# Seven stages instead of ten for a tile of rows through its expert, shifts on GpSimd, a second load

## The chip, the cores and the metric

The kernel runs on one core of one Trainium2 chip. The metric is the time of one execution on the device, in microseconds; the median of several runs is compared.

In the text, TensorE is the matrix engine (PE in the profile, PEld its loading of weights), VectorE is DVE, ScalarE is ACT, GpSimd is POOL, and SyncE (SP) issues most transfers. Each engine works through its own queue in order; where an instruction needs something of another engine or of a transfer, it waits, and everything behind it in that queue waits too.

## What is computed

Two layers over 6250 rows of 512 numbers: a graph layer (mean over incoming edges, two products, a norm over all rows, relu), and a mixture of eight experts of which each row uses two.

```python
x = x + gnn(layernorm(x), edge_index, W_l, b_l, W_r, gamma, beta)
x = x + ffn(layernorm(x)[None], ...)[0]

# gnn(x):
agg = segment_sum(x[src], dst)
h = (agg / maximum(cnt, 1)[:, None]) @ W_l.T + b_l + x @ W_r.T
h = (h - mean(h, 0)) * rsqrt(var(h, 0) + EPS) * gamma + beta
return relu(h) + x

# ffn(t):  D, H, E, K = 512, 256, 8, 2
logits = gelu(t @ Wg1 + bg1) @ Wg2 + bg2
topv, topi = top_k(softmax(logits), K);  topv = topv / sum(topv)
h = einsum('td,edh->eth', t, W1) + b1[:, None]
h = gelu(ln(h, g1, be1))
h = einsum('eth,ehg->etg', h, W2) + b2[:, None]
h = gelu(ln(h, g2, be2))
o = einsum('eth,eho->eto', h, W3) + b3[:, None]
out = einsum('te,eto->to', cw, o)      # cw: the two weights of a row
```

## The kernel before

**First part (to about 1226 us of the profile).** Rows are normalised and written to memory, edges are gathered by indirect transfers, summed by products with selection matrices, and multiplied with W_l and W_r. The change does not touch it.

**Tokens.** The 6250 rows are 49 tiles of 128 ("tokens"), in seven groups of seven. For each tile: two loads (`token_load`), the batch norm on VectorE (`token_scale`, L822 and L823), the residual on ScalarE (`token_shift`, L828), the sum and its statistics on VectorE (`token_sum`, L834 and L784), which also stores the sum to `out` as the value to which the experts will add (L835), the layer norm on ScalarE (`token_norm`, L804), transposes (`token_turn`, L846), and the gate (`token_gate`, `token_logits`). The two groups that come first are done ahead of the experts (`ahead`); the others go along with them, at most one tile in a step.

**Routing.** `route(q)` is a generator that finds for a group the two experts of each row, their weights (with an exponential on ScalarE, L920) and a slot for each, in pieces on VectorE that are put into the steps (`do`, `late`). Rows are then scattered by GpSimd (`send`, L868) to `xs_d`, a list of tiles of 128 rows, each tile of one expert. A row in `xs_d` has 528 columns (RW): 512 values, the row's number, eight weights and padding.

**Experts.** There are 102 tiles of slots in the main run (MOST), each through ten stages. `run(s, ...)` is one step. It issues, in this order of the program and so of every queue:

| place in a step | function, line | tile | engine |
|---|---|---|---|
| loads, four tiles ahead | `job_load` L1071 | to s+3 | SP |
| turn of the rows, copy to `xT` | `job_turn` L1086, L1088 | s | TensorE, ScalarE |
| turns of normed layers, gelu | `layer_turn` L1113, L1116 | s-3, s-6 | TensorE, ScalarE |
| scatter-add to `out` | `job_out` L1140 | s-9 | GpSimd |
| bias of W3 | `job_bias` L1132 | s-8 | VectorE |
| token work of VectorE | `token_scale`, `token_sum` | | VectorE |
| shifts of the last step's statistics | `shifts` L799 | | VectorE |
| norms | `layer_norm` L804 | s-2, s-5 | ScalarE |
| weighing | `job_weigh` L1136 | s-8 | ScalarE |
| pieces of the routing, row scatters | `do` | | VectorE, GpSimd |
| W1, its bias, statistics | `layer` L1096, L1099, L784 | s-1 | TensorE, VectorE |
| W2, its bias, statistics | `layer` | s-4 | TensorE, VectorE |
| W3 | `job_product` L1125 | s-7 | TensorE |
| a token's turn and gate | L846, L855 | | TensorE |
| scales | `scales` L794, L795 | | VectorE, GpSimd |

The order is written out by hand (`tc.manual_schedule`). A norm needs a scale, (var + EPS)^-0.5, and a shift, -mean times the scale. `scales`, at the end of a step, adds EPS on VectorE (L794) and takes the power on GpSimd (L795). `shifts`, in the middle of the next step, makes the product on VectorE (L799). `mv` holds them, three columns (tokens, first layer, second layer) by three numbers.

`job_turn` also copies the row's number, as an integer, and the weight of the tile's expert out of the loaded tile `xe` (four buffers) into `to` and `cw` (14 buffers each); the scatter takes `to` as its offsets, the weighing `cw` as its factor. `oe` has three buffers. Scatter-adds to `out` are in order: each waits for the one before it to land, as two tiles may hold the same row. After the last tile, ten more steps empty the stages.

Of the kernel before, what the change touches and what calls it, by code (L numbers as in the profile page):

```python
# [28 lines left out]
def gnn_moe_kernel(ctx: ExitStack, tc: tile.TileContext, x, src, dst, wlT, b_l, wrT, gamma, beta,  # L29
# [736 lines left out]
    def no_tokens(a):  # L766

        nc.vector.memset(a, 0.0)
        nc.vector.memset(a[:, D:D + 1], OOB)
        return a  # L770

    JOBS = {}

    class Step:
# [14 lines left out]
        def scales(self):  # L789
            if self.used:  # L790
                lo, hi = min(self.used), max(self.used) + 1
                assert hi - lo == len(self.used)
                self.part = self.mv[:, lo:hi]
                nc.vector.tensor_scalar(self.part[:, :, 1], self.part[:, :, 1], EPS, None, op0=OP.add)  # L794
                nc.gpsimd.tensor_tensor(self.part[:, :, 1], self.part[:, :, 1], mhalf[:, :hi - lo], op=OP.pow)  # L795

        def shifts(self):
            if self.used:
                nc.vector.scalar_tensor_tensor(self.part[:, :, 2], self.part[:, :, 0], -1.0,  # L799
                                               self.part[:, :, 1], op0=OP.mult, op1=OP.mult)  # L800
                self.used = []
# [80 lines left out]
    def route(q):  # L882
# [36 lines left out]
        nc.vector.tensor_tensor(s[:, 2:4], s[:, 0:2], s[:, None, 0].to_broadcast([P, 2, n]), op=OP.subtract)  # L919
        nc.scalar.activation(s[:, 2:4], s[:, 2:4], AF.Exp)  # L920
# [4 lines left out]
        nc.vector.tensor_copy(t2[:, :n, D], tok[:, g[0]:g[0] + n])  # L925
# [6 lines left out]
        nc.vector.tensor_add(s[:, 0], s[:, 2], s[:, 3])  # L932
        nc.vector.reciprocal(s[:, 1], s[:, 0])
        nc.vector.tensor_tensor(s[:, 2:4], s[:, 2:4], s[:, None, 1].to_broadcast([P, 2, n]), op=OP.mult)
# [131 lines left out]
    def job_load(p):  # L1066
        sl, e = JOBS[p]
        at = nc.values_load(sl, engines=[SP_], min_val=0, max_val=SLOTS,
                            skip_runtime_bounds_check_because="a tile's number, or SLOTS")
        xe = sb.tile([P, RW], F32, name="xe", bufs=4)  # L1070
        ld = nc.sync.dma_start(xe, xs_d[ds(at, 1)].rearrange("o p c -> p (o c)"))  # L1071
        tc.add_to_no_dep_group("full", ld.ins)
        XE[p] = xe

    def job_turn(p):
        xe = XE.pop(p)
# [69 lines left out]

    flat = [(q, j) for q in range(NQ) for j in range(len(groups[q]))]
# [14 lines left out]
    def ahead(i):  # L1162
# [10 lines left out]
        if i:  # L1173
            STEP[i - 1].shifts()
# [21 lines left out]
    def run(s, prev, lo, hi, moves=False, do=(), late=()):  # L1196
# [28 lines left out]
        tprev.shifts()  # L1225
        prev.shifts()
        for lag in (2, 5):
# [42 lines left out]
    with tc.manual_schedule():  # L1270
# [31 lines left out]
        STEP[n - 1].shifts()  # L1302
# [9 lines left out]
        tprev.shifts()  # L1312
# [53 lines left out]
        for s in range(MOST, MOST + 10):  # L1366
            prev = run(s, prev, 0, MOST)
    with tc.If(flag > 0), tc.manual_schedule():
        prev = Step()
        for s in range(MOST, SLOTS + 10):  # L1370
# [38 lines left out]
```

## Time and profile before

| what | us |
|---|---|
| median of 6 runs | 2039.19 (2034.93 to 2047.4) |
| the profiled execution | 2032.26 |
| its span, first to last instruction | 2030.5 |
| first turn of a tile in the expert part | 1309.90 |
| first scatter-add of results | 1375.98 |
| last turn of a tile | 1966.41 |
| last scatter-add | 2020.12 |

Busy time of each engine in stretches of the expert part, in us, with the clock granted to TensorE as a share of full speed:

| stretch | length | TensorE | VectorE | ScalarE | GpSimd | clock | DMA share |
|---|---|---|---|---|---|---|---|
| 1310 to 1340 | 30 | 22.98 | 25.47 | 13.81 | 7.27 | 0.67 | 0.50 |
| 1340 to 1375 | 35 | 33.78 | 23.75 | 22.44 | 13.27 | 0.92 | 0.44 |
| 1380 to 1752 | 372 | 352.40 | 304.00 | 271.41 | 189.96 | 0.98 | 0.68 |
| 1752 to 1838 | 86 | 73.72 | 58.55 | 49.36 | 55.22 | 0.95 | 0.61 |
| 1838 to 2031 | 193 | 157.81 | 94.49 | 105.16 | 75.39 | 0.92 | 0.44 |

A line of the page's groups gives the source line, the engine, the operation, output and input, the count, then busy time and the mean of one, then the engine's idle time just before and what ended it. A line of the timeline gives start, duration, engine, line, and in brackets the idle time ahead of it. A line of the waits gives who waited for whom: total, times, longest.

### The profile page before, as it was taken

The numbers are of one execution on the slowest core, as the hardware profiler recorded it, in microseconds if no ns is written. First come the engines' busy times: TensorE is split into PE (matmuls) and PEld (weight loads), VectorE is DVE, ScalarE is ACT, GpSimd is POOL, SyncE is SP. The second block draws the span as 40 slices with busy tenths as digits, with TensorE's granted clock in tenths as the row PEclk, the third lists the DMA queues.
The fourth block names the chain that finished last, engine by engine and source line by source line (L and its number), as shares of the span: only waits on it lengthen the run. The fifth ranks groups of instructions, "written<-read, shape, count | busy, mean of one in ns | idle before, by whom it ended". The sixth has DMA issues, their size and how long they took to land. (4 is left out here: it accounts for less than half of the span.)

```text
span 2030.5 us, 23976 instructions
## 1 busy us (share of the span) xinstructions
PE 1863.8 (92%) x6268; PEld 1033.3 (51%) x6268; DVE 1091.0 (54%) x2577; ACT 667.9 (33%) x1284; POOL 1212.0 (60%) x1229
## 2 busy tenths in 40 slices
PE   5877999999999999999999995588999999989993
PEld 2433444444444444444444443366767676666761
DVE  5652434334434434343344336878787878765661
ACT  3420101101010001011010014457777777756662
POOL 1427777777777777777777751335454646474442
PEclk9988999999999999999999996589999999999997
DMA  7968888878788888889888765646676767566532
GB/s 248 300 213 275 256 241 244 250 240 249 243 241 256 278 259 274 260 269 311 280 265 286 239 194 183 210 171 168 170 190 162 207 147 200 105 154 122 96 59 35
DMA packets 183185, 434.09 MB, mean 214 GB/s; under 512 B 32484, under 2 KB 38638, under 8 KB 182626
## 3 DMA queue, kind: packets, MB, share of 16 engines
q0 software_dynamic: 91040, 274.90, 49.0%
q1 hardware_dynamic: 91606, 156.69, 22.9%
q8 instruction: 56, 0.92, 0.2%
q10 hardware_dynamic: 396, 0.87, 0.1%
q14 instruction: 87, 0.71, 0.1%
HBM read 331.22 MB, written 104.20 MB: 214 GB/s over the span
## 5 line engine op out<-in xcount | busy, mean ns | idle before, releaser
L636 POOL DMA_INDIRECT xg<-xn_d,scol x832 | 795.1, 956 | 260.0 <-issue 123.9
L643 PE MATMUL pa<-xg,sel 128*128 128x512 f32 x1664 | 788.0, 596 | 20.7 <-DMA y_d<-xg 18.0
L643 PEld LDWEIGHTS pa<-xg,sel 128*128 128x128 f32 x1664 | 306.3, 190 | 364.4 <-issue 350.5
L1140 POOL DMA_INDIRECT out<-oe,to x102 | 165.6, 1624 | 196.6 <-DMA out<-oe,to 45.0
L528 ACT ACTIVATE sq<-dt 128x512 f32<-128x512 f32 x49 | 29.5, 602 | 557.4 <-DVE dt L526 281.2
L795 POOL TENSOR_TENSOR mv<-mv,mhalf 128x2 f32<-128x2 f32 (+2 forms) x121 | 106.1, 877 | 178.2 <-DVE mv L794 163.9
L1096 PE MATMUL pm<-w1s,xT 128*128 x816 | 207.8, 400 | 4.8 <-DVE hn L1099 4.8
L1125 PE MATMUL po<-w3s,hT 128*128 x408 | 197.4, 607 | 12.7 <-DVE oe L1132 12.4
L562 DVE TENSOR_REDUCE ss<-sel 128x128 f32<-128x2304 f32 x49 | 200.5, 4092 | 0.6 <-issue 0.6
L432 PE MATMUL ph<-wl,xT 128*128 128x512 f32 x392 | 199.8, 592 | 0.7 <-ACT xT L427 0.7
L1096 PEld LDWEIGHTS pm<-w1s,xT 128*128 128x128 f32 x816 | 154.6, 200 | 25.1 <-DVE hn L1099 5.9
L1116 ACT ACTIVATE hT<-pt,gbe 128x128 f32<-128x128 f32 x408 | 154.2, 462 | 1.9 <-PE pt L1113 1.8
L507 DVE TENSOR_SCALAR rc<-pt 128x1 f32<-128x1 f32 x49 | 7.8, 158 | 270.7 <-PE pt L586 270.7
L804 ACT ACTIVATE hn<-hn,mv 128x256 f32<-128x256 f32 x204 | 111.9, 599 | 108.0 <-DVE mv L799 107.7
L868 POOL DMA_INDIRECT xs_d<-t,pos x98 | 101.6, 1037 | 40.8 <-issue 23.8
L556 DVE TENSOR_TENSOR sel<-jrow_p,dcol 128x2304 f32<-128x2304 f32 x49 | 124.4, 2539 | 0.0
L432 PEld LDWEIGHTS ph<-wl,xT 128*128 128x128 f32 x392 | 74.4, 190 | 94.2 <-issue 93.3
L526 DVE TENSOR_TENSOR dt<-ph,shift 128x512 f32<-128x512 f32 x25 | 17.3, 692 | 192.2 <-PE ph L432 192.2
L567 ACT ACTIVATE ag<-pa,rc 128x512 f32<-128x512 f32 x49 | 33.7, 687 | 248.9 <-PE pa L643 248.9
L1125 PEld LDWEIGHTS po<-w3s,hT 128*128 128x128 f32 x408 | 76.2, 192 | 75.8 <-issue 53.9
L524 DVE TENSOR_TENSOR dt<-ph,xo 128x512 f32<-128x512 f32 x24 | 16.6, 692 | 182.4 <-PE ph L432 182.4
L1096 PE MATMUL pm<-w2s,hT 128*128 x408 | 104.8, 379 | 0.0
(307 smaller groups left out, 2246.0 us busy)
## 6 DMA issues: line engine op xcount, KB each, us to landing
xe<-xs_d SPq DMA_DIRECT2D x102, 264.0 KB
xg<-xn_d,scol POOLq DMA_INDIRECT x832, 3.9
d_d<-dt SPq DMA_DIRECT2D x49, 256.0 KB
dt<-d_d SPq DMA_DIRECT2D x49, 256.0 KB
xt<-in_x SPq DMA_DIRECT2D x24, 512.0 KB
xn_d<-xt SPq DMA_DIRECT2D x24, 512.0 KB
xy<-y_d SPq DMA_DIRECT2D x48, 256.0 KB
xt<-in_x SPq DMA_DIRECT2D x48, 256.0 KB
```

Source lines behind the costliest of these rows:

```text
L432: nc.tensor.matmul(p, xT[:, k, :], w[:, k, :], start=start and k == 0, stop=stop and k == KD - 1)
L556: nc.vector.tensor_tensor(SEL[t], jrow_p[:, None, :].to_broadcast([P, KS, P]), dcol[:, t // TG, (t % TG) * KS:(t % TG + 1) * KS, None].to_ ...
L562: nc.vector.tensor_reduce(ss, SEL[t].rearrange("p k j -> p j k"), AX.X, OP.add)
L636: nc.gpsimd.indirect_dma_start(out=xg, out_offset=None, in_=xn_d[:, :], in_offset=bass.IndirectOffsetOnAxis(ap=scol[:, t // TG, c:c + 1], ...
L643: nc.tensor.matmul(PA[t], SEL[t][:, k, :], xg, start=(k == 0), stop=(k == last))
L795: nc.gpsimd.tensor_tensor(self.part[:, :, 1], self.part[:, :, 1], mhalf[:, :hi - lo], op=OP.pow)
L804: nc.scalar.activation(out_, in_, AF.Identity, bias=scale_shift[1], scale=scale_shift[0])
L868: st = nc.gpsimd.indirect_dma_start(out=xs_d.rearrange("n p c -> (n p) c"), out_offset=bass.IndirectOffsetOnAxis(ap=at, axis=0), in_=rows_ ...
L1096: nc.tensor.matmul(pm, lhs[:, k, :], w[:, k, ds(e, 1), :].rearrange("p o h -> p (o h)"), start=(k == 0), stop=(k == kk - 1))
L1116: nc.scalar.activation(hT[:, k, :], pt[:, k, :], AF.Gelu, bias=gb[:, 2 * i + 1:2 * i + 2], scale=gb[:, 2 * i:2 * i + 1])
L1125: nc.tensor.matmul(po, hT[:, k, :], w3s[:, k, ds(e, 1), :].rearrange("p o h -> p (o h)"), start=(k == 0), stop=(k == KH - 1))
L1140: st = nc.gpsimd.indirect_dma_start(out=out[:, :], out_offset=bass.IndirectOffsetOnAxis(ap=to[:, 0:1], axis=0), in_=OE.pop(p), in_offset=N ...
```

## The change

Stages are drawn together: W1 is issued in the step of its turn (tile s), W2 in the step of its turn (s-2), W3 goes ahead of W1 and W2 (s-5), and its bias and weighing follow in the same step. The second turn is of tile s-4, the scatter-add of s-6. Seven steps empty the stages, not ten.

The shift is made on GpSimd behind the power, as is the addition of EPS; VectorE only negates the mean. `shifts` is gone.

The loaded tile comes in two transfers: 512 values into `xe`, the last 16 columns into `ev` (14 buffers), which the scatter and the weighing read directly; the row's number is stored there as an integer from the start. The two copies are gone.

The exponential of the routing is a power of e on GpSimd, of one number instead of two. The tile without tokens, written once at the start, uses another buffer.

```diff
@@ no_tokens
-        nc.vector.memset(a[:, D:D + 1], OOB)
+        nc.vector.memset(a[:, D:D + 1].bitcast(I32), int(OOB))
...
+    euler = wts.tile([P, GMAX], F32, name="euler")
+    nc.vector.memset(euler, 2.718281828459045)
@@ Step.scales
-                nc.vector.tensor_scalar(self.part[:, :, 1], self.part[:, :, 1], EPS, None, op0=OP.add)
-                nc.gpsimd.tensor_tensor(self.part[:, :, 1], self.part[:, :, 1], mhalf[:, :hi - lo], op=OP.pow)
-
-        def shifts(self):
-            if self.used:
-                nc.vector.scalar_tensor_tensor(self.part[:, :, 2], self.part[:, :, 0], -1.0,
-                                               self.part[:, :, 1], op0=OP.mult, op1=OP.mult)
-                self.used = []
+                mean, var, shift = (self.part[:, :, i] for i in range(3))
+                nc.vector.tensor_scalar(shift, mean, -1.0, None, op0=OP.mult)
+                nc.gpsimd.tensor_scalar(var, var, EPS, None, op0=OP.add)
+                nc.gpsimd.tensor_tensor(var, var, mhalf[:, :hi - lo], op=OP.pow)
+                nc.gpsimd.tensor_tensor(shift, shift, var, op=OP.mult)
@@ route
-        nc.vector.tensor_tensor(s[:, 2:4], s[:, 0:2], s[:, None, 0].to_broadcast([P, 2, n]), op=OP.subtract)
-        nc.scalar.activation(s[:, 2:4], s[:, 2:4], AF.Exp)
+        nc.vector.tensor_sub(s[:, 3], s[:, 1], s[:, 0])
+        nc.gpsimd.tensor_tensor(s[:, 3], euler[:, :n], s[:, 3], op=OP.pow)
...
-        nc.vector.tensor_add(s[:, 0], s[:, 2], s[:, 3])
-        nc.vector.reciprocal(s[:, 1], s[:, 0])
-        nc.vector.tensor_tensor(s[:, 2:4], s[:, 2:4], s[:, None, 1].to_broadcast([P, 2, n]), op=OP.mult)
+        nc.vector.tensor_scalar(s[:, 0], s[:, 3], 1.0, None, op0=OP.add)
+        nc.vector.reciprocal(s[:, 2], s[:, 0])
+        nc.vector.tensor_mul(s[:, 3], s[:, 3], s[:, 2])
@@ job_load
-        xe = sb.tile([P, RW], F32, name="xe", bufs=4)
-        ld = nc.sync.dma_start(xe, xs_d[ds(at, 1)].rearrange("o p c -> p (o c)"))
-        tc.add_to_no_dep_group("full", ld.ins)
-        XE[p] = xe
+        xe = sb.tile([P, D], F32, name="xe", bufs=4)
+        ev = sb.tile([P, RW - D], F32, name="ev", bufs=14)
+        for a, lo, hi in ((xe, 0, D), (ev, D, RW)):
+            ld = nc.sync.dma_start(a, xs_d[ds(at, 1), :, lo:hi].rearrange("o p c -> p (o c)"))
+            tc.add_to_no_dep_group("full", ld.ins)
+        XE[p] = xe, ev
@@ job_turn
-        to = sb.tile([P, 1], I32, name="to", bufs=14)
-        cw = sb.tile([P, 1], F32, name="cw", bufs=14)
-        nc.vector.tensor_copy(to, xe[:, D:D + 1])
-        nc.vector.tensor_copy(cw, xe[:, D + 1:D + 1 + E][:, ds(e, 1)])
-        EV[p] = e, to, cw
+        EV[p] = e, ev[:, 0:1].bitcast(I32), ev[:, 1:1 + E][:, ds(e, 1)]
@@ ahead
-        if i:
-            STEP[i - 1].shifts()
@@ run
-        for i, lag in ((0, 3), (1, 6)):
+        for i, lag in ((0, 2), (1, 4)):
             if on(lag):
                 layer_turn(s - lag, i)
-        if on(9):
-            job_out(s - 9)
-        if on(8):
-            job_bias(s - 8)
+        if on(6):
+            job_out(s - 6)
...
-        tprev.shifts()
-        prev.shifts()
-        for lag in (2, 5):
+        if on(5):
+            job_product(s - 5)
+            job_bias(s - 5)
+        for lag in (1, 3):
             if on(lag):
                 layer_norm(s - lag)
...
-        if on(8):
-            job_weigh(s - 8)
+        if on(5):
+            job_weigh(s - 5)
         for f in do:
             f()
-        if on(1):
-            layer(s - 1, 0, step)
-        if on(4):
-            layer(s - 4, 1, step)
-        if on(7):
-            job_product(s - 7)
+        if on(0):
+            layer(s, 0, step)
+        if on(2):
+            layer(s - 2, 1, step)
@@ the start of the token work
             if i == 3:
-                no = sb.tile([P, RW], F32, name="xe", bufs=4)
-                nc.sync.dma_start(xs_d[SLOTS], no_tokens(no))
+                nc.sync.dma_start(xs_d[SLOTS], no_tokens(t2s[1][:, 0, :]))
@@ the last steps
-        for s in range(MOST, MOST + 10):
+        for s in range(MOST, MOST + 7):
             prev = run(s, prev, 0, MOST)
```

More of the change, by code (lines that the diff above doesn't have):

```diff
@@ L924, in route @@
         nc.vector.tensor_add(m, mm[:, 0], mm[:, 1])
-        nc.vector.tensor_copy(t2[:, :n, D], tok[:, g[0]:g[0] + n])
+        nc.vector.tensor_copy(t2[:, :n, D].bitcast(I32), tok[:, g[0]:g[0] + n])
         nc.vector.memset(t2[:, :, D + 1 + E:], 0.0)
@@ L1069, in job_load @@
                             skip_runtime_bounds_check_because="a tile's number, or SLOTS")
[L1070 to L1073 removed]
+        xe = sb.tile([P, D], F32, name="xe", bufs=4)
[4 more added lines that the diff above has]
+        XE[p] = xe, ev
     def job_turn(p):
[L1076 removed]
+        xe, ev = XE.pop(p)
         e = nc.values_load(JOBS[p][1], engines=[PE_, DVE_, ACT_], min_val=0, max_val=E - 1,
                            skip_runtime_bounds_check_because="an expert's number")
[L1079 to L1083 removed]
+        EV[p] = e, ev[:, 0:1].bitcast(I32), ev[:, 1:1 + E][:, ds(e, 1)]
         pt = ps.tile([P, KD, P], F32, name="pt", bufs=3)
@@ L1301, in gnn_moe_kernel @@
         token_scale(*flat[n])
-        STEP[n - 1].shifts()
         token_norm(*flat[n - 1])
@@ L1311, in gnn_moe_kernel @@
         token_scale(*flat[n + 1])
-        tprev.shifts()
         token_norm(*flat[n])
@@ L1369, in gnn_moe_kernel @@
         prev = Step()
-        for s in range(MOST, SLOTS + 10):
+        for s in range(MOST, SLOTS + 7):
             prev = run(s, prev, MOST, SLOTS)
```

## The prediction

> **What bounds the kernel now.** I read the page first, then the last part of the chain of waits, the scatter's own rows, one undisturbed step of TensorE, and last what TensorE and ScalarE waited for. The change touches the expert part, which begins with the first turn of a tile at 1309.90 us, and a little of the token work from 1226 on; the sums before that stay.
>
> The end is set by the scatter-adds of results. The page's group, the scatter's landing, and the last rows of GpSimd's timeline (start, duration, idle time before and what ended it):
>
> ```profile
> L1140 POOL DMA_INDIRECT out<-oe,to x102 | 165.6, 1624 | 196.6 <-DMA out<-oe,to 45.0
> ```
> ```profile
> DMA to landing us min/median/max: 3.1/5.0/7.6
> ```
> ```profile
> 1999.88 1.59 POOL L1140 DMA_INDIRECT out<-oe,to  x1 [3.22 <-DMA out<-oe,to]
> 2005.47 1.53 POOL L1140 DMA_INDIRECT out<-oe,to  x1 [4.00 <-DMA out<-oe,to]
> 2010.60 1.53 POOL L1140 DMA_INDIRECT out<-oe,to  x1 [3.60 <-DMA out<-oe,to]
> 2016.27 1.54 POOL L1140 DMA_INDIRECT out<-oe,to  x1 [4.14 <-DMA out<-oe,to]
> 2020.12 1.54 POOL L1140 DMA_INDIRECT out<-oe,to  x1 [2.32 <-DMA out<-oe,to]
> ```
>
> Each scatter starts about 0.77 us after the one before has landed: the scatters are a chain of their own, whoever has finished earlier. Scatter 68 starts at 1838.10, scatter 101 at 2020.12: 182.0 us for 33, or 5.52 us each. From scatter 55 (1757.88) on it is 5.70 each, and most already follow on the landing. The last tile is turned at 1966.41, so 53.7 us are drain.
>
> One step without tokens, on TensorE, in the same stretch:
>
> ```profile
> 1864.19 0.60 PE L1086 MATMUL pt<-identx,xe 128*128 128x128 f32 x4
> 1864.63 0.60 PE L1113 MATMUL pt<-identx,hn 128*128 128x128 f32 x4
> 1865.06 1.89 PE L1096 MATMUL pm<-w1s,xT 128*128 x8
> 1866.79 1.03 PE L1096 MATMUL pm<-w2s,hT 128*128 x4
> 1867.65 1.88 PE L1125 MATMUL po<-w3s,hT 128*128 x4
> ```
>
> It repeats every 5.18 us without a gap, slightly faster than the scatters' 5.52; they fall behind it and at last hold it up. With tokens a step takes 7.26 us (turns at 1614.31, 1621.56, 1628.82), and there TensorE leads. From 1380 to 1752 it is busy 352.40 of 372 us. What it waited for from 1380 to 1890, and ScalarE's longest wait from 1380 on:
>
> ```profile
> PE pt L846 <- ACT t L804: 12.0, 6, 2.8
> PE pt L1113 <- ACT hn L804: 6.0, 6, 2.0
> ```
> ```profile
> ACT hn L804 <- DVE mv L799: 104.6, 59, 4.8
> ```
> ```profile
> 1592.72 0.82 ACT L828 ACTIVATE xt<-xt,nm,mr 128x512 f32<-128x512 f32 x1
> 1596.26 1.09 ACT L804 ACTIVATE hn<-hn,mv 128x256 f32<-128x256 f32 x2 [2.72 <-DVE mv L799]
> ```
>
> The reader is to see that the norms wait for VectorE's shift (L799), which is queued behind the next step's token work, although GpSimd had its power ready at 1592.77.
>
> **The change, part by part.**
>
> *Ten stages to seven.* In step s the scatter of tile s-6 is issued, not of s-9. The place in GpSimd's queue is the same: ahead of the row scatters and the scales. So at any late step the chain of scatters is three tiles ahead, and 3 x 5.52 = 16.6 us fall off the end. Bounds: 15.5 (TensorE's 5.18 a step decides) and 17.1 (5.70).
>
> *Cost of filling.* The tiles in flight are done earlier, so TensorE has more behind it at any step: one W1 (1.72), two W2 (0.87 each), two W3 (1.72 each), two tiles' second turn and one tile's first (three times 0.43, half of the four transposes' 0.87): 1.72 + 1.74 + 3.44 + 1.3 = 8.2 us. It hides in idle time of TensorE while the pipe fills: 7.0 us from 1310 to 1340 (busy 22.98 of 30, at a granted clock of 0.67) and 1.2 to 1375. VectorE is busy 25.47 of the first 30 us and stretches those steps. Without cover it costs 8.2; covered, nothing. I take 3, since 8.2 of idle time stand against work that the clock of 0.67 makes longer.
>
> *Order within a step.* W3 now lies between the turns and W1. The copy of xT takes 0.59 and ends 1.28 us after the turn's start (1864.88 against 1864.19); W1 starts at 0.87 + 1.72 = 2.6. The two gelus of the first layer end some 0.75 later and W2 starts at 4.3. So W1 and W2 need not wait: nothing, with 1.3 us to spare. Bias and weighing go behind W3 in the same step: W3 ends near 2.7, bias 0.69, weighing 0.7, done at 4.1 of 5.18; in VectorE's queue the bias goes behind the token work (four operations of 0.68 to 0.69), and the scatter that needs it comes a step later. What loses cover is the norm: before, W3's 1.72 us lay between W2's end and the next step. From W1's end (1861.77) to the power's start (1864.45) it is 2.7 us. In the new step W1 ends 0.7 before the next turn, so GpSimd starts 2.0 after it.
>
> *Shifts on GpSimd.* VectorE loses the shift (0.15 us) and swaps adding EPS for a negation. GpSimd gets an add and a product, not seen in the trace. Nearest row, the power: 0.54 us for one column, 0.70 for two, 0.88 for three, and 1.15 directly behind a scatter. Some 0.17 a column is the power's own work, so 0.37 is the lower bound, 0.88 the upper, 1.15 behind a scatter. I take 0.5, as an add is cheaper than a power. Then the scales are ready at 2.0 + 0.5 + 0.7 + 0.5 = 3.7 in the pure step; ScalarE gets there at 2.56, ends two norms (1.10) and the weighing (0.73) at 5.6, and its next copy is due at 5.87. Nothing on the path, by 0.3 us; beyond that, xT still has 1.3 us of W3's cover. In token steps nothing waits for VectorE's queue any more: at 1592.77 + 1.0 the norms could start at 1593.8 instead of 1596.26. Of the 18.0 us of TensorE's waits above I take 8 back (0 to 18), as some will turn into waits for GpSimd.
>
> The power beside VectorE's product of two SBUF tiles (L822) took 0.75 us at 1586.10, against 0.72 at 1864.45 with none beside it. The Trainium skill, "SBUF — State Buffer", section "SBUF: two separate sides", says that a GpSimd operation and a VectorE operation with two SBUF inputs exclude each other for the whole instruction. By that rule each of the two new operations could wait 0.69 us, so the scales come 1.4 us later in a token step, about half of what the norms win there; 8 would shrink to 4 and the sum would be -14.6. By the row it stays as taken.
>
> *GpSimd in the last group.* From 1752 to 1838 it is busy 55.22 of 86 us, scatters and rows alternate, and the chain of waits goes through its row scatters. Two more operations of 0.5 in 13 steps, hidden where a landing is waited for: 0 to 8 us, I take 3, because most of those scatters still started 0.77 to 0.82 after a landing.
>
> *A second load.* SP issues 102 small loads more. The queue's packets average 22.9% x 16 x 2030.5 / 91606 = 81 ns; 128 of them on 16 engines are 0.65 us of each engine per tile, 9 points of DMA share. Landings take about 5.1 at shares of 0.6 to 0.7 and 4.8 in the drain at 0.44, so 0.1 us a scatter: 0 to 4 us over the 43 that bind, I take 2. In return the xe buffer is freed by TensorE alone; SP waited 172.9 us for the copy (L1082), at a lead of 10 to 20 us, so no gain. The two copies (0.15 each) leave VectorE, which is not the bound: nothing.
>
> *Softmax as a power on GpSimd, token steps before the experts.* ScalarE loses 14 table loads of 1.28 us, of which two or three lie on the path (TensorE idled 1.79 us at 1285.57 behind one). VectorE, busy 16 to 19 of every 20 us from 1240 to 1300, loses 17 shifts of 0.15; against it stands 1.0 us more from sum to norm at the end of two runs of tokens. I take -2 (-5 to +2).
>
> Sum: -16.6 + 3 - 8 + 3 + 2 - 2 = -18.6 us. The profiled execution took 2032.26 us (span 2030.5 and 1.8 around it), so it would take 2013.7. The median of the runs shown, 2039.19, lies 6.9 above that execution; the forecast for the median is 2020.6 us.
>
> **The rivals.**
>
> *More than that.* All 18 us of the norms' waits come back, the fill is free, the small costs vanish: -16.6 - 18 - 5 = -39.6, 1999.6 us. For it speaks that 59 waits for L799 go; against it, that the token steps have other edges (xe cost 4.9 once).
>
> *It evens out.* The fill costs its 8.2, nothing comes back at the norms: -16.6 + 8.2 + 2 + 3 + 2 = -1.4, 2037.8 us. For it speaks TensorE's 352 of 372 busy.
>
> *GpSimd becomes the bound (slower).* In a token step its queue holds 0.74 from a landing to the scatter's start, the scatter 1.62, two row scatters of 1.0 with 0.3 ahead of each, and the power 0.94: 5.9 of 7.26 us. The two new operations fit while they are below 0.68 each. At 1.15 each, the row behind a scatter, the step is 0.9 too long; 70 row scatters make 35 such steps, 33 us: -18.6 + 33 = +14.4, 2053.6 us. Against it: behind row scatters the power took 0.94, hardly more than alone.
>
> **How the numbers follow.** The forecast gets 0.55, the larger gain 0.14, evening out 0.13, GpSimd 0.18. The forecast's own range is 2010 to 2032; taking in the bounds of fill and norms and both milder rivals, 2001 to 2040, which leaves out nearly all of the slower case and half of the larger gain's low end. About 0.3%, 6.1 us, is what a measurement can tell from none: faster, below 2033.1, is the forecast, the larger gain and a little of evening out: 0.72; same 0.10; slower 0.18.
>
> **What would show it.** Right: the last scatter comes some 37 us after the last turn, not 53.7; scatters stay 5.5 apart; ScalarE's norms no longer wait for VectorE; pure steps stay at 5.18. Wrong: pure steps above 5.3 with TensorE waiting for hn (the norms have lost their cover), token steps above 7.3 with GpSimd busy throughout, or scatters above 5.7 apart in the drain (the small loads). The tail's 16.6 fails if scatters are held by something else than the landing.

## The result and the profile after

The changed kernel takes 2052.82 us (median of 20 runs, 2043.99 to 2057.24) against 2039.3 of the kernel before on the same chip (46 runs): ratio 1.0061, 95% interval [1.0049, 1.0073]. The forecast was 2020.6 and a gain.

The two profiled executions, cut at the same points (starts of the tiles' turns, L1086 before and L1083 after; the last product of L432 ends a part that the change doesn't touch). A profile is of one execution: 2032.26 us before, 7.0 below its median, and 2051.13 after, 1.7 below, so the table's sum of 18.9 is more than the 13.5 between the medians. The untouched part alone lies between 1221.6 and 1227.0 in the fourteen profiles that are not of e10 to e13 (whose chip is slow there, see below).

| stretch | before, us | after, us | difference |
|---|---|---|---|
| start to the last product of L432 | 1222.4 | 1225.7 | +3.3 |
| to the first turn (token work alone) | 87.5 | 94.9 | +7.4 |
| turn 0 to turn 10 (fill) | 68.5 | 73.3 | +4.8 |
| turn 10 to turn 64 | 373.3 | 388.9 | +15.6 |
| turn 64 to turn 101 (last) | 214.7 | 217.4 | +2.7 |
| last turn to last scatter (drain) | 53.7 | 39.1 | -14.6 |
| last scatter to the end | 10.4 | 10.1 | -0.3 |
| span | 2030.5 | 2049.4 | +18.9 |

The drain came near its forecast (14.6 us shorter, 16.6 expected). The page's group of the scatter-add and the last scatters on GpSimd's timeline (start, duration, idle time ahead and what ended it):

```profile
L1137 POOL DMA_INDIRECT out<-oe,ev x102 | 167.2, 1639 | 159.5 <-ACT hn L803 35.0
```
```profile
2024.35 1.63 POOL L1137 DMA_INDIRECT out<-oe,ev  x1 [2.82 <-DMA out<-oe,ev]
2029.91 1.55 POOL L1137 DMA_INDIRECT out<-oe,ev  x1 [3.93 <-issue]
2035.39 1.55 POOL L1137 DMA_INDIRECT out<-oe,ev  x1 [3.93 <-issue]
2039.27 1.55 POOL L1137 DMA_INDIRECT out<-oe,ev  x1 [2.33 <-POOLq L1358]
```

They are still some 5.5 apart (5.68 each from scatter 68 to 101, where it was 5.52). But the chain starts later: the turns have lost 23 us on their way from the first to the last, and 7 before it. What TensorE, VectorE and ScalarE waited for in the changed kernel from 1310 to 1960 (total us, times, longest), one engine after the other:

```profile
PE pt L845 <- ACT t L803: 26.1, 21, 3.1
PE pt L1110 <- ACT hn L803: 12.4, 13, 1.9
PE pl L928 <- DVE t L925: 5.1, 4, 1.5
```
```profile
DVE oe L1129 <- PE po L1122: 94.7, 53, 7.9
```
```profile
ACT hn L803 <- POOL mv L800: 130.4, 78, 4.0
```

In the same stretch of the kernel before, TensorE's first two waits were 18.6 and 6.2 us, and ScalarE's norms waited 92.1 us for the shift. So the norms do not wait less; they wait more, and for GpSimd. (How much of that is the shifts' new place is seen only in e1 and e9.) New is that VectorE stands 94.7 us in front of W3's bias (L1129). What that does is seen best where tokens end, in a step that all groups have. TensorE of the changed kernel from turn 21 to turn 22, then VectorE:

```profile
1473.36 0.66 PE L1083 MATMUL pt<-identx,xe 128*128 128x128 f32 x4
1474.70 1.98 PE L1122 MATMUL po<-w3s,hT 128*128 x4
1476.52 1.89 PE L1093 MATMUL pm<-w1s,xT 128*128 x8
1478.25 1.03 PE L1093 MATMUL pm<-w2s,hT 128*128 x4
1480.48 0.40 PE L928 MATMUL pl<-gm,lower 128*128 128x56 f32 x2 [1.21 <-DVE t L925]
1480.94 0.61 PE L1083 MATMUL pt<-identx,xe 128*128 128x128 f32 x4
```
```profile
1473.95 0.17 DVE L797 TENSOR_SCALAR mv<-mv 128x2 f32<-128x2 f32 x1
1476.78 0.69 DVE L1129 TENSOR_TENSOR oe<-po,b3s 128x512 f32<-128x512 f32 x1 [2.66 <-PE po L1122]
1477.39 0.21 DVE L910 TENSOR_REDUCE gs<-pl 128x7 f32<-128x56 f32 x1
...
1480.12 0.22 DVE L923 TENSOR_TENSOR gm<-gmm 128x56 f32<-128x56 f32 x1
```

VectorE has nothing to do for 2.66 us, because the next thing in its queue is the bias of W3, and W3 has only begun (1474.70); the routing (L910 to L925), whose input is there, starts 4.03 us after the turn. Before, the bias stood at the head of the step and the routing started 1.44 after it. Its mask reaches TensorE late, and the step is 7.58 long in place of 6.13. There are five such steps (8-9, 21-22, 35-36, 49-50, 63-64): 7.57, 7.58, 7.58, 7.58, 7.85 against 6.13 each, 7.5 us together.

The norms, in the step from 1641.83 on, GpSimd, then ScalarE, then TensorE:

```profile
1642.31 1.65 POOL L1137 DMA_INDIRECT out<-oe,ev  x1 [3.93 <-ACT tt L847]
1644.27 1.44 POOL L867 DMA_INDIRECT xs_d<-t,pos  x1 [0.30 <-issue]
1646.01 0.99 POOL L867 DMA_INDIRECT xs_d<-t,pos  x1 [0.31 <-issue]
1647.00 0.30 POOL L798 TENSOR_SCALAR mv<-mv 128x3 f32<-128x3 f32 x1
1647.38 0.89 POOL L799 TENSOR_TENSOR mv<-mv,mhalf 128x3 f32<-128x3 f32 x1
1648.35 0.19 POOL L800 TENSOR_TENSOR mv<-mv 128x3 f32<-128x3 f32 x1
1648.58 1.09 ACT L803 ACTIVATE hn<-hn,mv 128x256 f32<-128x256 f32 x2 [3.23 <-POOL mv L800]
1650.43 0.66 PE L845 MATMUL pt<-identx,t 128*128 128x128 f32 x4 [2.69 <-ACT t L803]
```

The statistics were ready at 1641.66 (the negation, L797). The scatter ahead in GpSimd's queue had itself waited 3.93 us, then came two row scatters, and only 5.3 us after the statistics the three small operations. They are cheap (0.30, 0.89, 0.19); what costs is where they stand.

The same is seen without tokens. Steps without tokens begin at 5.18 us, but from turn 86 to turn 99 they last 5.35 to 5.77 (in e1, with the shifts on VectorE, they are 5.18 up to turn 94). In the step from 1928.51 the statistics are ready at 1930.34, GpSimd stands at a scatter that starts at 1931.03, the three operations end at 1934.00, and the norm starts at 1934.03; TensorE, nowhere idle for long, is held up at the second turn (0.93 us in place of 0.60).

### The profile page after: what moved, and what is told of

Read it like the earlier page. It is cut to its first block, busy times and chain, and to the rows that moved or that the text cites. A ratio compares the mean times of both kernels' runs of the same rounds, so it can differ in the third digit from the quotient of the medians.

```text
span 2049.4 us, 24603 instructions
## 1 busy us (share of the span) xinstructions
PE 1866.9 (91%) x6268; PEld 1030.6 (50%) x6268; DVE 1048.2 (51%) x2251; ACT 650.6 (32%) x1263; POOL 1293.3 (63%) x1472
## 5 line engine op out<-in xcount | busy, mean ns | idle before, releaser
L1137 POOL DMA_INDIRECT out<-oe,ev x102 | 167.2, 1639 | 159.5 <-ACT hn L803 35.0
L1122 PE MATMUL po<-w3s,hT 128*128 x408 | 203.0, 621 | 1.6 <-DVE oe L1129 1.6
L432 PE MATMUL ph<-wl,xT 128*128 128x512 f32 x392 | 199.8, 592 | 0.7 <-ACT xT L427 0.7
L1093 PE MATMUL pm<-w1s,xT 128*128 x816 | 197.0, 385 | 3.7 <-DVE hn L1096 2.0
L1129 DVE TENSOR_TENSOR oe<-po,b3s 128x512 f32<-128x512 f32 x102 | 70.6, 692 | 133.3 <-PE po L1122 122.9
L432 PEld LDWEIGHTS ph<-wl,xT 128*128 128x128 f32 x392 | 74.4, 190 | 94.2 <-issue 93.3
L798 POOL TENSOR_SCALAR mv<-mv 128x2 f32<-128x2 f32 (+2 forms) x119 | 48.0, 403 | 111.7 <-DVE mv L787 111.4
L524 DVE TENSOR_TENSOR dt<-ph,xo 128x512 f32<-128x512 f32 x24 | 16.6, 692 | 184.2 <-PE ph L432 184.2
```

The source lines that it names most:

```text
L432: nc.tensor.matmul(p, xT[:, k, :], w[:, k, :], start=start and k == 0, stop=stop and k == KD - 1)
L1093: nc.tensor.matmul(pm, lhs[:, k, :], w[:, k, ds(e, 1), :].rearrange("p o h -> p (o h)"), start=(k == 0), stop=(k == kk - 1))
L1122: nc.tensor.matmul(po, hT[:, k, :], w3s[:, k, ds(e, 1), :].rearrange("p o h -> p (o h)"), start=(k == 0), stop=(k == KH - 1))
L1129: nc.vector.tensor_add(oe, OE[p], b3s[:, ds(e, 1), :].rearrange("p o h -> p (o h)"))
L1137: st = nc.gpsimd.indirect_dma_start(out=out[:, :], out_offset=bass.IndirectOffsetOnAxis(ap=to[:, 0:1], axis=0), in_=OE.pop(p), in_offset=N ...
```

## The experiments

Two theories. *Queue*: W3's bias, now in the middle of VectorE's queue, holds up what stands behind it (the shifts if they are there, and the routing). *Cover*: W3 no longer lies behind W2 and gives the norms no time. Rivals: the scales' place in GpSimd's queue, the routing's power, the second load.

"Prelude" is from L432's last product to the first turn, "way" from the first turn to the last, "drain" from there to the last scatter, each from one profile; ratios are to the kernel before on the same chip. The profiled execution is not the median one: it took 11 us more than the median in e8, 7 in e2, 6 in e6 and 20 in e10 (in all four the slowest), 16 less in e13 and 4 less in e1. No kernel was profiled twice, so a difference of a few us between two rows is not told from chance.

| run | ratio, 95% interval | prelude | way | drain |
|---|---|---|---|---|
| before | 1 | 87.5 | 656.5 | 53.7 |
| changed | 1.0061 [1.0049, 1.0073] | 94.9 | 679.6 | 39.1 |
| e1 shifts back | 1.0036 [1.0022, 1.0051] | 88.0 | 672.2 | 38.4 |
| e2 Exp back | 1.0050 [1.0033, 1.0068] | 90.6 | 688.0 | 37.5 |
| e4 ten stages | 1.0072 [1.0053, 1.0091] | 91.8 | 664.5 | 53.3 |
| e5 stages alone | 1.0056 [1.0040, 1.0072] | 86.8 | 681.8 | 38.6 |
| e6 shifts first | 1.0051 [1.0032, 1.0069] | 90.1 | 681.5 | 38.8 |
| e7 W3 first | 1.0142 [1.0115, 1.0168] | 89.8 | 676.3 | 53.2 |
| e8 eight stages | 0.9946 [0.9927, 0.9965] | 91.1 | 661.3 | 43.2 |
| e9 shifts alone | 1.0068 [1.0044, 1.0092] | 92.7 | 665.0 | 52.7 |
| e10 bias late | 0.9946 [0.9906, 0.9987] | 93.7 | 671.4 | 37.9 |
| e11 bias late, shifts back | 0.9982 [0.9949, 1.0016] | 90.2 | 664.7 | 36.9 |
| e12 eight, load, power | 0.9877 [0.9827, 0.9927] | 88.6 | 653.5 | 41.8 |
| e13 load alone | 0.9944 [0.9912, 0.9977] | 91.0 | 655.9 | 52.7 |
| e14 W3 first, bias late | 1.0075 [1.0060, 1.0089] | 89.6 | 671.2 | 53.3 |
| e15 eight, load | 0.9915 [0.9895, 0.9935] | 87.6 | 653.3 | 42.8 |
| e16 seven mended | 0.9987 [0.9977, 0.9996] | 87.6 | 665.4 | 38.4 |
| e17 W2 last | 1.0058 [1.0042, 1.0074] | 87.8 | 666.9 | 50.3 |

Four chips: the kernel before took 2030.8 (e1 to e5), 2031.7 (e6 to e9), 2232.0 (e10 to e13) and 2033.1 us (e14 to e17). On the third, nearly all of the excess lies ahead of L432's last product (1396 to 1434 us in the four profiles, in place of 1222), so those four ratios are blunt; the expert part takes no longer than elsewhere (e13), and its stretches are compared. The prelude scatters by 2 us either way in runs that change nothing in it (86.8 to 91.1).

### One part taken back at a time (e1, e2, e4, e5)

*e1, shifts and EPS on VectorE again*

```diff
-nc.vector.tensor_scalar(shift, mean, -1.0, None, op0=OP.mult)
-nc.gpsimd.tensor_scalar(var, var, EPS, None, op0=OP.add)
-nc.gpsimd.tensor_tensor(var, var, mhalf[:, :hi - lo], op=OP.pow)
-nc.gpsimd.tensor_tensor(shift, shift, var, op=OP.mult)
+nc.vector.tensor_scalar(self.part[:, :, 1], self.part[:, :, 1], EPS, None, op0=OP.add)
+nc.gpsimd.tensor_tensor(self.part[:, :, 1], self.part[:, :, 1], mhalf[:, :hi - lo], op=OP.pow)
...
+        tprev.shifts()
+        prev.shifts()
         for lag in (1, 3):
```

> The changed kernel with the shifts and the adding of EPS on VectorE again; the power alone stays on GpSimd. If the scales' new place is the cause (all three operations in GpSimd's queue, behind a scatter that waits for its landing and behind the row scatters; ScalarE's hn waited 152.8 us for POOL mv L800), the steps before the last group lose some 15 to 20 us and the time falls to about 2035, with turn 64 some 462 us after the first turn in place of 442 before and 462 now turning back to about 445. If the order of the stages is the cause (W3 at the start of the step has taken the norm's cover), it stays at 2045 to 2055. If the routing's power is the cause, it stays at about 2045 to 2050.

2038.44 us. It lands between: 5 us better in the ratio, not 15 to 20, and the two intervals just touch. Nor did the steps before the last group come back: turn 64 is 465.5 us after the first turn (462.2 in the changed kernel, 445 expected). What is shorter is the last group, 206.7 against 217.4, and the prelude.

*e2, the exponential on ScalarE again*

```diff
-nc.gpsimd.tensor_tensor(s[:, 3], euler[:, :n], s[:, 3], op=OP.pow)
+nc.scalar.activation(s[:, 3], s[:, 3], AF.Exp)
```

> The changed kernel with the softmax's exponential on ScalarE again. If the routing's power in GpSimd's queue is the cause (17.9 us in which GpSimd stood at L919 waiting for VectorE, and 7 us of the way to the first turn), the time falls by 15 to 20 us, to about 2035. If the scales' place is the cause, it falls by 5 at most, by what the first turn comes earlier (about 2048). If the order of the stages is, by 5 at most too.

2043.99 us; the intervals of this ratio and the changed kernel's overlap. The routing's power is not the cause.

*e4, ten stages in the old order, all else as changed* (lags 3, 6, 9, 8 and W1, W2, W3 at the step's end, as in the kernel before)

> The changed kernel with ten stages again, in the order of before; all else as changed. The drain grows by 14 to 17 us. If the order of the stages is what lengthens the steps, they come back to their old length (some 15 us) and the time stays near 2050 or below it, with ScalarE's norms waiting less for the scales than 152.8 us. If the scales' place or the routing's power is the cause, the long steps stay and the drain is added: 2060 to 2068.

2045.72 us, a ratio of 1.0072: the way is 8 us longer than before, the prelude 4. So the rest of the change costs something by itself. But the way is also 15 shorter than the changed kernel's, about what the drain lost: the new order buys nothing.

*e5, the seven stages alone* (shifts on VectorE, Exp on ScalarE, one load and the two copies; the rest of the diff as it is)

> Seven stages in the new order alone: shifts on VectorE, the exponential on ScalarE, one load of a tile. If the order of the stages costs what it saves, 2040 to 2050. If it is sound and the other parts are what costs, the drain is 14 to 16 us shorter and little stands against it: 2023 to 2030, and it beats the kernel before.

2042.86 us. The order alone makes the kernel slower by 0.56%: the drain is 15.1 shorter, and the way 25.3 longer, 7.2 of it up to turn 10 and 21.8 from there to turn 64, with 3.7 won back after it. The costs do not add up: the rest of the change costs 0.72% with the old order (e4) and next to nothing on top of the new one (1.0061 against 1.0056). One reason shows in the steps: in the middle of a run of tokens they are 7.57 here, where the shifts stand behind the bias, and 7.26 in the changed kernel where nothing else disturbs them.

### Queue or cover (e6, e7, e8, e9)

*e6: e5 with the shifts ahead of the bias*

```diff
+        tprev.shifts()
+        prev.shifts()
         if on(5):
             job_product(s - 5)
             job_bias(s - 5)
-        tprev.shifts()
-        prev.shifts()
```

> Seven stages alone (shifts on VectorE, Exp on ScalarE, one load), but the shifts of the step before stand ahead of W3's bias in VectorE's queue instead of behind it. If the bias, which waits in the middle of VectorE's queue until W3 is done (40.8 us in 28 waits from 1310 to 1780), is what makes the norms late, the way from the first to the last turn falls from 681.8 us to about 662 to 668, the fill of 7 staying, and the time to 1.0056 - 0.007 to 0.009, that is 0.997 to 0.999 of before. If the norms are late because W3 no longer lies behind W2 in the step, little changes: 678 to 682 and a ratio near 1.005.

2042.57 us, 1.0051, way 681.5: no gain that can be told from e5. Steps in the middle of a run of tokens, 7.57 in e5, are 7.26 here where nothing else disturbs them, but the five steps with the routing stay at 7.58 to 7.85, and others grow to 8 or 9. As it was put (the shifts), the queue theory falls; the routing is left in it.

*e7: the kernel before, only W3 and its bias moved*

```diff
-        if on(8):
-            job_bias(s - 8)
...
+        if on(8):
+            job_product(s - 8)
+            job_bias(s - 8)
         tprev.shifts()
         prev.shifts()
...
-        if on(7):
-            job_product(s - 7)
```

> The kernel before with ten stages; only W3 and its bias are moved from the end of one step to the place between the turns and W1 of the next, as in the changed kernel (a third buffer for hT1, eleven for to and cw). No tile is further ahead than before, so there is no fill and no shorter drain. If W3's place is the cause of the longer steps, the way from the first to the last turn grows from 656.5 by 15 to 22 us and the ratio is about 1.008 to 1.011. If the cause is the tighter chain of one tile (seven stages), it stays within 4 us of before: ratio 0.998 to 1.002.

2058.06 us, 1.0142: with no tile further ahead, no fill and no shorter drain, W3's place alone costs more than the whole change. In the profile 19.8 us of it lie on the way. The steps show how. Within a run of tokens its steps are 7.57 and not 7.26. Here the step from turn 33 to turn 34, the timeline's rows of TensorE, VectorE and ScalarE that form a ring:

```profile
1553.94 0.66 PE L1086 MATMUL pt<-identx,xe 128*128 128x128 f32 x4
1555.27 1.98 PE L1125 MATMUL po<-w3s,hT 128*128 x4
1557.30 0.69 DVE L1132 TENSOR_TENSOR oe<-po,b3s 128x512 f32<-128x512 f32 x1 [0.17 <-PE po L1125]
1557.90 0.15 DVE L799 SCALAR_TENSOR_TENSOR mv<-mv 128x3 f32<-128x3 f32 x1
1558.09 1.09 ACT L804 ACTIVATE hn<-hn,mv 128x256 f32<-128x256 f32 x2 [1.41 <-DVE mv L799]
1559.09 0.80 ACT L804 ACTIVATE t<-xt,mv 128x512 f32<-128x512 f32 x1
1559.94 0.66 PE L846 MATMUL pt<-identx,t 128*128 128x128 f32 x4
1560.53 1.05 PE L855 MATMUL pg<-tt,wg1s 128*16 128x128 f32 x8
1561.51 0.66 PE L1086 MATMUL pt<-identx,xe 128*128 128x128 f32 x4
```

Each follows on the one above it: W3 (behind the second turns and the logits), its bias, the shift, two norms, the token's norm, the token's turn and gate, the next tile's turn. 1561.51 - 1553.94 is 7.57. The power was ready at 1557.58 (L795, 1556.69 + 0.89); the shift stood behind the bias.

*e8: eight stages, the old order kept*

```diff
-        for i, lag in ((0, 3), (1, 6)):
+        for i, lag in ((0, 3), (1, 5)):
...
-        if on(9):
-            job_out(s - 9)
-        if on(8):
-            job_bias(s - 8)
+        if on(7):
+            job_out(s - 7)
+        if on(6):
+            job_bias(s - 6)
...
-        if on(4):
-            layer(s - 4, 1, step)
-        if on(7):
-            job_product(s - 7)
+        if on(3):
+            layer(s - 3, 1, step)
+        if on(5):
+            job_product(s - 5)
```

> The kernel before with eight stages in its old order: W2 and W3 in the step of their transposes, W1 a step behind its turn, W3 last in the step, bias and weighing a step later. The drain loses 2 x 5.5 = 11 us; at any step one more W2, two W3 and one second turn lie ahead: 0.87 + 3.44 + 0.43 = 4.7 us of fill. If the order is the cause, the steps stay as before (first to last turn 656 to 662) and the ratio is about 0.996 to 0.998. If the tighter chain of a tile is the cause, that way grows by 10 us or more and the ratio is 1.000 to 1.005.

2021.47 us, 0.9946: faster than the kernel before. W2 and W3 run in the step of their transposes here (in the changed kernel W3 comes a step after them), so a tighter chain at these two is not what costs; W1 in the step of its turn, which the changed kernel has as well, no run tests by itself. The drain is 10.5 shorter (two scatters). The way is 4.8 longer, but that agrees with the expected fill of 4.7 by chance: only 1.7 of it lies up to turn 10, and the profile is of the slowest of the eight executions (2032.7 us).

*e9: the scales' operations alone*

```diff
-nc.vector.tensor_scalar(self.part[:, :, 1], self.part[:, :, 1], EPS, None, op0=OP.add)
-nc.gpsimd.tensor_tensor(self.part[:, :, 1], self.part[:, :, 1], mhalf[:, :hi - lo], op=OP.pow)
+nc.vector.tensor_scalar(shift, mean, -1.0, None, op0=OP.mult)
+nc.gpsimd.tensor_scalar(var, var, EPS, None, op0=OP.add)
+nc.gpsimd.tensor_tensor(var, var, mhalf[:, :hi - lo], op=OP.pow)
+nc.gpsimd.tensor_tensor(shift, shift, var, op=OP.mult)
```

> The kernel before with only the three small operations of the scales moved (EPS and shift to GpSimd, the negation to VectorE). If the scales' place in GpSimd's queue behind scatters costs by itself, the way from the first to the last turn grows by 8 to 15 us over 656.5 and the ratio is 1.004 to 1.008, as with ten stages and all other parts (1.0072). If it costs nothing alone and the load or the routing's power are behind that, the ratio is 0.998 to 1.002.

2046.7 us, 1.0068: the way is 8.5 longer, the prelude 5.2. (This kernel, like e13, e15 and e16, also takes the routing's exponential of one number, on ScalarE, and has the changed kernel's buffer for the tile without tokens.) GpSimd, ScalarE and TensorE in one place of it:

```profile
1502.39 0.99 POOL L867 DMA_INDIRECT xs_d<-t,pos  x1 [0.30 <-issue]
1503.38 0.28 POOL L798 TENSOR_SCALAR mv<-mv 128x3 f32<-128x3 f32 x1
1503.74 1.35 POOL L799 TENSOR_TENSOR mv<-mv,mhalf 128x3 f32<-128x3 f32 x1
1505.18 0.55 POOL L800 TENSOR_TENSOR mv<-mv 128x3 f32<-128x3 f32 x1
1505.76 1.09 ACT L803 ACTIVATE hn<-hn,mv 128x256 f32<-128x256 f32 x2 [2.49 <-POOL mv L800]
1507.61 0.66 PE L845 MATMUL pt<-identx,t 128*128 128x128 f32 x4 [1.82 <-ACT t L803]
```

The statistics were ready at 1502.21 (L797). A row scatter first, then three operations in a row, 2.35 us, where the kernel before has one on GpSimd (0.88) and the shift on VectorE. From 1310 to 1960 TensorE waits 30.1 us for the token's norm, where it waited 18.6 before.

### The bias moved, the load alone (e10 to e13)

*e10: the changed kernel, one edit* (e11 the same with the shifts of e1)

```diff
             job_product(s - 5)
-            job_bias(s - 5)
...
-        if on(5):
-            job_weigh(s - 5)
         for f in do:
             f()
+        if on(5):
+            job_bias(s - 5)
+            job_weigh(s - 5)
```

> The changed kernel with one thing moved: W3's bias and the weighing stand behind the routing's parts of the step, not ahead of them, so that VectorE does the routing while W3 runs. If the bias that waits in VectorE's queue holds up the routing, and through it TensorE (1.21 us at L928 in the step that begins at 1473.36, 7.58 us long where it was 6.13), the five steps 8-9, 21-22, 35-36, 49-50 and 63-64 come back to about 6.2 from 7.6 to 7.9, the way from the first to the last turn falls by 7 to 10 us from 679.6 and the ratio to about 1.002 from 1.0061. If the cause is that W3 no longer covers the norms, those steps and the ratio stay (1.005 to 1.007).

The five steps with the routing are 6.13 again, all of them (expected 6.2), and the way is 8.2 us shorter, 671.4. The ratio, 0.9946 [0.9906, 0.9987], is from the blunt chip; that the edit removes the changed kernel's whole loss is not shown by it. The five steps are shown, 7.5 us together: e11 has them at 6.13 as well.

> The same with the shifts on VectorE, ahead of the bias (seven stages, the second load and the routing's power kept). By the queue theory both things that stood behind the bias, shifts and routing, are free: steps of 7.57 go back to 7.26 and those of 7.6 to 7.9 to 6.2, first to last turn about 660 in place of 672.2, ratio 0.996 to 0.999. By the cover theory as with the shifts back alone: 1.003 to 1.005.

Way 664.7 against e1's 672.2 (about 660 was expected), the five steps at 6.13 again; in the middle of a run of tokens they are 7.25 to 7.7, with several of 8 to 12, and not 7.26 throughout. The ratio is not told from 1.

*e12: eight stages in the old order with the second load and the routing's power; e13: the kernel before with the second load alone*

> Eight stages in the old order (shifts on VectorE) together with the second load and the routing's power. If these two save VectorE's time as they seem to beside seven stages (1.0036 with them, 1.0056 without), the ratio falls from 0.9946 to about 0.992; if the small loads cost the scatters 2 us and the power another 2, it is 0.996.

> The kernel before with the second load alone (numbers and weights by a load of their own, no copies on VectorE). By the prediction's term +2 us: ratio 1.001. If the two copies at the head of VectorE's queue, which wait for the load's landing and the expert's number (28.4 us in 85 waits), were worth something, 0.997 to 0.999.

0.9877 and 0.9944, both on the blunt chip; e12's interval holds the 0.992 that was expected. Way and drain of e13 are those of before within 1 us, so its ratio rests on something that its profile doesn't show; a cost of the load of 2 us is seen neither in the ratio nor in these stretches.

### What is left beside the queue, and versions that win (e14 to e17)

*e14: e7 with bias and weighing behind shifts and routing* (the edit of e10 on e7)

> Ten stages, W3 first in the step, as in the run with W3 first (ratio 1.0142, first to last turn 676.3 us), but its bias and weighing stand behind the shifts and the routing's parts in VectorE's queue. If what waits behind the bias is the cause, the steps come back: first to last turn 656 to 662, ratio 1.000 to 1.004, the last steps of the runs of tokens 6.13 in place of 7.6 to 8.0. If the lost cover of the norms is the cause, it stays at 670 or more and the ratio at 1.009 or more.

1.0075 in place of 1.0142, and up to turn 64 the steps lose 10.0 us, not 20.3. The last steps of the runs of tokens are 6.13, 6.13, 6.13, 6.13 and 6.22. So up to turn 64, and by the ratio, the queue is about half of W3's price. Over the whole way it is a quarter: 671.2 us, which is where the cover theory had it, is 14.7 more than before and e7 19.8, as the last group is 5.2 longer here than in e7.

*e17: W2 and W3 exchanged, the bias in its old place*

```diff
+        if on(7):
+            job_product(s - 7)
         if on(4):
             layer(s - 4, 1, step)
-        if on(7):
-            job_product(s - 7)
```

> The kernel before with W2 and W3 exchanged on TensorE (W1, W3, W2), bias and all else in their old places. W2's norm loses W3's 1.72 us of cover, and nothing new waits in VectorE's queue. If the cover decides, first to last turn grows by 10 us or more over 656.5 and the ratio is 1.005 to 1.010. If the queue decides, it is 0.998 to 1.003.

1.0058 and a way 10.4 longer, the numbers that the cover theory had named. But TensorE's waits from 1310 to 1960 show that something else came in, first in e17, then in e14:

```profile
PE pt L846 <- ACT t L804: 19.8, 15, 3.8
PE po L1125 <- DVE oe L1132: 15.1, 27, 1.4
```
```profile
PE pt L846 <- ACT t L804: 28.0, 15, 4.4
PE po L1125 <- DVE oe L1132: 9.2, 12, 3.0
```

W3 runs earlier in the step and meets the bias that has not yet emptied its only PSUM buffer: 15.1 us in 27 waits, where the kernel before has 2.8 in 6. In e17 these 12.3 us more are enough for the whole growth of the way; the token's norm is hardly later (19.8 against 18.6). So e17 does not confirm the cover theory. In e14 both have grown, by 9.4 and 6.4. No run has a second buffer, which would part the two. That W3's place costs something beside the queue is shown; its division between the norms' cover and that buffer is open. In the changed kernel itself W3 waits for that buffer 1.6 us in all, so there the buffer is not the cause.

*e15: eight stages, old order, second load; e16: seven stages, new order, second load, shifts on VectorE, Exp on ScalarE, bias late*

> Eight stages in the old order and the second load, shifts on VectorE and Exp on ScalarE. Without the load the ratio was 0.9946; if the load saves VectorE the copies and their waits, 0.991 to 0.993; if it costs the scatters 2 us, 0.995 to 0.996.

> Seven stages in the new order with the second load, shifts on VectorE, Exp on ScalarE, and bias and weighing behind shifts and routing. If the queue theory holds, first to last turn is 660 to 666 (656.5 and the fill of 5 to 7), the drain 37 to 39, and the ratio 0.994 to 0.998, a little behind the eight stages. If the cover decides, the way stays at 672 or more and the ratio at 1.002 or more.

e15 takes 2016.0 us against 2033.1 on the same chip, 0.9915 [0.9895, 0.9935]: the best that was measured on a chip that can tell it, and faster than both kernels. Its way is 653.3, and 653.5 in e12 with the same load, against 661.3 without it (e8, from its slowest execution); the intervals of e8 and e15 still overlap a little. e16, the changed order with its bias mended, is 0.9987 [0.9977, 0.9996], just faster than before; e5 without the mending and the load was 1.0056. Its way (665.4) and drain (38.4) came as the queue theory had them, its ratio a little above the expected 0.994 to 0.998. It stays 12 us of way behind e15, 4.0 of them in the fill; what the rest is, no run shows.

## Why the prediction was wrong, point by point

Two steps of it failed: the order within a step, priced at nothing, and the norms' waits, priced at 8 us of gain. The tail came nearly as forecast, and these two, with the fill, ate it up.

- *The tail, -16.6.* Right in kind, a little too large: 14.6 in the changed kernel, under the lower bound of 15.5; 15.1 in e5, 10.5 for two stages in e8, scatters about 5.5 to 5.7 apart.
- *Filling, +3 (0 to 8.2).* Right in kind, mis-sized: 4.8, and 7.2 in e5; e7, with the same order and no fill, has 0.1 there.
- *Order within a step, "nothing, with 1.3 us to spare".* This step failed. It asked whether W1, W2 and the copy must wait, and what the bias stands behind; it did not ask what stands behind the bias. In VectorE's queue those are the shifts (ring of 7.57, e7) and the routing (7.58 in place of 6.13, 1.21 us of it TensorE's wait). It also tested the norms' lost cover in the pure step alone, and for token steps took the time at which the power was ready before, when W3 still lay behind W2. Priced at 0; e7 shows +1.4% [1.15, 1.68], 26 us between the medians and 19.8 on the profile's way, of which a quarter (way) to a half (ratio) goes with the bias moved (e14). In the changed kernel the bias moved gives back the five steps, 7 to 8 us of the 23.1 (e10). What the rest of W3's price is, cover or the single buffer, is open.
- *Norms' waits, -8.* Wrong in sign; this step failed too. It took away VectorE's queue and did not ask for GpSimd's: a scatter that waits, two row scatters, then three operations in series. Alone, e9, it costs 8.5 us of way and some 4 of prelude (five profiles with it have 90.6 to 94.9 there, thirteen without it 86.8 to 91.1). In the new order it costs less: 1.0061 against e1's 1.0036. The sum of ScalarE's waits does not measure it: 130.4 us in the changed kernel and 92.1 before, but 96.5 in e9, and 149.1 in e1, where the shifts are back on VectorE and stand behind the bias.
- *GpSimd's durations, 0.5 each.* The add took 0.29 in the median and the product 0.19, so the rival that GpSimd becomes the bound had its prices too high: its point of 0.68 was reached by single operations alone (add up to 0.82, product up to 0.74), and GpSimd is not busy throughout. That it named the time (2053.6, measured 2052.82) is luck: the mechanism that gave it was another.
- *The rule against the row.* The Trainium skill, "SBUF — State Buffer", "SBUF: two separate sides", has such operations exclude each other; the prediction went by the row. From 1330 on in the changed kernel the product took 0.19 in the median of 94 cases with none of VectorE's three two-input token operations beside it, and 0.61 in 9 with one; the power of three columns 0.89 (27) and 1.18 (5), that of two columns 0.72 in both (62 and 7). The rule's direction holds in this trace, but it meets one operation in ten: some 5 us of GpSimd's time in all.
- *GpSimd in the last group, +3.* Turn 64 to 101 grew by 2.7; in e5, without those operations, it fell by 3.7, in e1 by 8.0. But in e9, with them alone, it fell by 0.7, so the 3 is not shown as a price of theirs.
- *Second load, +2.* No such cost is seen, and perhaps a gain: e15 is 0.3% below e8, on different chips and with intervals that overlap, and with the one-number exponential besides. The two copies at the head of VectorE's queue, which the load removes, waited 27.4 us in 79 waits in e8. In e13 way and drain do not change.
- *Power of the routing, -2.* Not seen: e2 and the changed kernel are not told apart.
- *What would show it* worked in part: the drain (39.1) and the scatters were right. Two signs of being wrong came: token steps above 7.3, though with GpSimd at 57 to 60% and not busy throughout, and pure steps above 5.3 from turn 86 on, where the second turn waits for the norm, though there for GpSimd's place behind a scatter.

## What to carry to other kernels

When an instruction is moved within a step, go through each in-order queue twice: what is it behind, and what is now behind it; an instruction that waits in the middle of a queue delays all that follows, also what belongs to other work. Drawing stages together pays for each tile that the last chain gets ahead, and can be had without touching the order that the engines' waits have been fitted to (e8, e15). Here a small operation on another engine cost what stood ahead of it there, not its duration.

## What was not expected of the hardware

An idle time of 2 to 3 us on TensorE can cost twice. After the wait of 2.69 us at 1650.43 shown above, the granted clock (the number after the five engines' busy times) falls in the changed kernel from 1.00 to 0.63 for the next 4.6 us:

```profile
1641.00:1650.00 9.00, 6.74 (x34) 4.66 (x32) 6.75 (x17) 5.14 (x11) 6.20 (x7) 1.00 0.58 156
1650.40:1655.00 4.60, 4.57 (x23) 3.34 (x23) 0.77 (x2) 2.57 (x6) 3.83 (x6) 0.63 1.01 255
1655.00:1662.00 7.00, 7.00 (x38) 5.07 (x38) 4.76 (x16) 4.72 (x10) 1.73 (x2) 1.00 0.46 98
```

In e9 it is 0.59 for 7.7 us after 2.74 us of waiting, and W1's eight products take 3.78 us in place of 1.89. The length of the wait does not decide alone: in e15 it is 0.63 from 1722.00 to 1726.60 after a wait of 1.97, and in e5 it stays at 1.00 after waits of 3.01 and 2.98 (1514.34, 1613.62). The Trainium skill, "TensorE: Matmul & The Clock Gate", section "Why this matters for your kernels", asks for no gap above about 3 us; here 2.7 and less were enough in some cases. So a late norm can cost more than its wait. It is no part of the difference between the two kernels, though: the kernel before has such falls as well (0.63 from 1598.00 to 1602.60, after 2.76 us), and from 1380 to 1752 the clock is 0.98 in both.
